# Transposes of the next tokens laid between value projections, and a first batch sorted in wider spaced pieces

## Chip, core and metric

The kernel runs on one core of a Trainium2 chip. The metric is the time of the device for one execution, in microseconds (us), as the median of several runs. PE is the matrix engine (PEld its loading of stationary operands), DVE the vector engine, ACT the scalar engine, POOL GpSimd and SP the engine whose queue issues most of the transfers (DMA). All arithmetic is in 32-bit floats.

## What is computed

Two images `x` of 256 channels and 56 x 56 pixels go through a non-local convolution block, and are then read as 2 batches of 3136 tokens of 256 values for a layer of causal attention and a layer of experts. The change lies in the second and third part.

```python
def reference(x, ...):
    x = conv_block(x, ...)                      # non-local block, ReLU, residual
    t = to_tokens(x)                            # (2, 3136, 256)
    # attention: 4 heads of 64, causal
    q, k, v = split(layernorm(t) @ W_attn)
    att = softmax(where(causal, q @ k.T / 8, min))
    t = t + (att @ v) @ W_proj
    # experts: each token goes to the best 2 of 8
    xf = layernorm(t)
    probs = softmax(xf @ gate_w + gate_b)       # (tokens, 8)
    cw = the two largest of probs, zero elsewhere
    t = t + sum_e cw[:, e] * (gelu(xf @ W1[e] + b1[e]) @ W2[e] + b2[e])
    return from_tokens(t)
```

## The kernel before

**One order for all engines.** In the attention stage the order of instructions is set by hand. Attention is cut into steps; there are 200 for each batch, one for each block of 448 queries, pair of heads and tile of 128 keys. Ahead of each step, `between` adds some other work: at every odd step two pieces from a queue (gate, output projection, sorting, scattering, loads), at every even one some pieces of the projections for the next queries. A piece is what a Python generator issues up to its next `yield`. `yield True` counts as a piece, `yield False` says that there is nothing to do now, and the next generator in the queue is asked.

```python
def pull(n=1):
    while n > 0:
        for g in list(queue):
            r = next(g, None)
            if r is None:
                queue.remove(g)
                break
            if r is not False:
                n -= 1
                break
        else:
            return

def between(i, left):            # left: steps to the end of this block of queries
    # ... loads of W2 at the very end
    tick[0] += 1
    if tick[0] % 2:
        pull(2)
        return
    nb, s = (b, i + 1) if i + 1 < NB else (b + 1, 0)
    if nb < B and s < NS and (nb == b or left < NCH - QB // P - 2):
        rest = max(0, PARTS * (s + 1) - at[nb] - 1)
        for _ in range(2 * -(-rest // max(2, left))):
            if at[nb] + 1 < PARTS * (s + 1):
                step(nb)
```

**The projections.** 512 tokens (4 tiles) at a time, as ten pieces: two of transposes (two tiles each), four of queries and keys, four of values. The rows are normalised on POOL one pair ahead, transposed on PE into a bank of PSUM, and copied by ACT to `px`, which has two halves. All results go through the same two banks (`tag="m"`, two buffers).

```python
pm = pool(whole, "m", bufs=2, space=PSUM)
bg = pool(whole, "bg", bufs=2)

def project_qkv(b, qT, kT, v, px):
    # todo: the pairs of tiles in order
    def normalise():
        # ...
        xn = bg.tile([P, 2, C], F32, tag="xn", ...)
        for a in range(m):
            nc.gpsimd.tensor_scalar(xn[:k, a], ts[b][:k, n + a, :C], mean, rstd, ALU.subtract, ALU.mult)
        ready[n] = xn

    normalise()
    for s in range(NS):
        # ...
        xT = px[:, s % 2]
        for n, m, k in pairs(first, end):                  # transposes
            xn = ready.pop(n)
            normalise()
            tp = bank(f"xp_{b}_{n}", (P, NH, 2 * P))
            # ... nc.tensor.transpose into tp
            nc.scalar.copy(xT[:, :, o : o + wp], tp[:, :, :wp])
            yield s
        for which in range(2):                             # queries, keys
            for hp in range(NH):
                ps = bank(f"qk_{b}_{s}_{which}_{hp}")
                # ... two matmuls with wat and xT
                nc.scalar.copy(to[:, s * QB : s * QB + w], ps[:, :w])
                yield s
        for n in range(first, end):                        # values
            ps = bank(f"v_{b}_{n}", (P, 512))
            # ... two matmuls with xT and wv, two copies by ACT
            yield s
```

The columns of `wv` beside the values hold the centred gate `gwc`, which two small matmuls (`gp`) and four DVE operations make before anything else of this layer. `wT`, which the gate needs once, takes a buffer of the tag `xn` too.

**The sorting** (`dispatch`) gives each token of a batch its place among the experts' blocks: some forty small DVE operations, a few at a time, with `small_piece` between them; then `hot` selects biases for `bp`, and each tile of rows is normalised by DVE (`xr`) and scattered to `x_slots` by two indirect transfers from POOL. The first batch is sorted during the attention of the second.

```python
def small_piece():
    yield True
    if b == 0:
        yield True
# ...
hot = g1.tile([E, w], F32, tag="hot", ...)
nc.vector.tensor_tensor(hot, eb[:E, :w], row.to_broadcast([E, w]), ALU.is_equal)
yield from small_piece()
if b:
    yield True
bp = bank(f"bp_{b}", (P, KH, w))
# ... matmuls of bp, a copy, small_piece
for n in range(NCH):
    # ... xr on DVE
    for k in range(2):
        nc.gpsimd.indirect_dma_start(out=xds[b], out_offset=idxs[b][:kk, k, n : n + 1], in_=xr[:kk], ...)
        yield True
        if b == 0:
            yield False
sent[b] = True
```

After its last scatter the first batch's queue loads `w1s`, in the place of that batch's rows, and the first rows for the experts (`xb_f_first`).

Of the kernel before, what the change touches and what calls it, by code (L numbers as in the profile page):

```python
# [13 lines left out]
ALU = mybir.AluOpType  # L14
# [13 lines left out]
def conv_attn_moe_kernel(  # L28
# [47 lines left out]
    nc = tc.nc  # L76
    P = 128
# [349 lines left out]
    def layer1(nm, general):  # L427

        with ExitStack() as whole:
# [7 lines left out]
            def bank(name, shape=(P, 512)):  # L437
                return pm.tile(list(shape), F32, tag="m", name=f"{name}_{nm}")


            gp = bank("gp")
            gpc = gp[:, :E]
            for c in range(NH):
                nc.tensor.matmul(gpc, ones, gw[:, c], start=(c == 0), stop=(c == NH - 1))
            for c in range(NH):
                nc.vector.scalar_tensor_tensor(gwc[:, c], gpc, -1.0 / C, gw[:, c], ALU.mult, ALU.add)
                nc.vector.tensor_copy(
                    wv[:, c, :, HS:], gwc[:, c].rearrange("p (h e) -> p h e", h=HEADS)
                )

            def project_gate():

# [20 lines left out]
            def project_qkv(b, qT, kT, v, px):  # L473

                todo = deque(p for s in range(NS) for p in pairs(s * QB // P, min(NCH, (s + 1) * QB // P)))
                ready = {}

                def normalise():
                    if not todo:
                        return  # L480
                    n, m, k = todo.popleft()
                    xn = bg.tile([P, 2, C], F32, tag="xn", name=f"xn_{nm}{b}_{n}")
                    for a in range(m):
                        nc.gpsimd.tensor_scalar(  # L484
                            xn[:k, a], ts[b][:k, n + a, :C],
                            ts[b][:k, n + a, MEAN : MEAN + 1], ts[b][:k, n + a, RSTD : RSTD + 1],
                            ALU.subtract, ALU.mult,
                        )
                    ready[n] = xn

                normalise()
                for s in range(NS):
                    w = min(QB, N - s * QB)
                    first, end = s * QB // P, -(-(s * QB + w) // P)
                    xT = px[:, s % 2]
                    for n, m, k in pairs(first, end):
                        xn = ready.pop(n)
                        normalise()
                        tp = bank(f"xp_{b}_{n}", (P, NH, 2 * P))
                        for a in range(m):  # L500
                            for c in range(NH):
                                nc.tensor.transpose(
                                    tp[:, c, a * P : a * P + k],
                                    xn[:k, a, c * P : (c + 1) * P],
                                    ident[:k, :k],
                                )
                        o, wp = n * P - s * QB, (m - 1) * P + k
                        nc.scalar.copy(xT[:, :, o : o + wp], tp[:, :, :wp])  # L508
                        yield s
                    for which in range(2):  # L510
                        for hp in range(NH):
                            ps = bank(f"qk_{b}_{s}_{which}_{hp}")
                            d0 = which * C + hp * P
                            for c in range(NH):
                                nc.tensor.matmul(  # L515
                                    ps[:, :w],
                                    wat[:, c, d0 : d0 + P],
                                    xT[:, c, :w],
                                    start=(c == 0),
                                    stop=(c == NH - 1),  # L520
                                )
                            to = kT[hp] if which else qT[:, hp]
                            nc.scalar.copy(to[:, s * QB : s * QB + w], ps[:, :w])
                            yield s
                    for n in range(first, end):
                        k = chunk(n)
                        ps = bank(f"v_{b}_{n}", (P, 512))
                        o = n * P - s * QB
                        for c in range(NH):
                            nc.tensor.matmul(  # L530
                                ps[:k, : C + E],
                                xT[:, c, o : o + k],
                                wv[:, c].rearrange("p h d -> p (h d)"),
                                start=(c == 0),
                                stop=(c == NH - 1),
                            )
                        half = (C + E) // NH
                        for hp in range(NH):
                            nc.scalar.copy(
                                v[hp][:k, n].rearrange("p a d -> p (a d)"),  # L540
                                ps[:k, hp * half : (hp + 1) * half],
                            )
                        yield s

                    full = [n for n in range(first, end) if chunk(n) == P]
                    for f, e, k in ((first, first + len(full), P), (first + len(full), end, chunk(end - 1))):
                        for hp in range(NH if f < e else 0):
                            c0 = C + 2 * hp * LH
                            nc.vector.tensor_tensor(
                                ts[b][:k, f:e, c0 : c0 + 2 * LH].rearrange("p n (a e) -> p n a e", a=2),  # L550
                                v[hp][:k, f:e, :, HS:],
                                ts[b][:k, f:e, SLOT : SLOT + 1].unsqueeze(3).to_broadcast(
                                    [k, e - f, 2, LH]
                                ),
                                ALU.mult,
                            )
                read[b] = True
# [349 lines left out]
            def dispatch(b):  # L907
# [5 lines left out]

                def small_piece():

                    yield True
                    if b == 0:
                        yield True

                def small(name, last=E, dt=F32):  # L920
# [172 lines left out]
                hot = g1.tile([E, w], F32, tag="hot", name=f"hot_{nm}{b}")  # L1093
                nc.vector.tensor_tensor(hot, eb[:E, :w], row.to_broadcast([E, w]), ALU.is_equal)
                yield from small_piece()
                if b:
                    yield True
                bp = bank(f"bp_{b}", (P, KH, w))
                for k in range(KH):
# [7 lines left out]
                for n in range(NCH):  # L1107
                    kk = chunk(n)
                    xr = (scatter_rows[0] if b else bg).tile(
                        [P, width], F32, tag="xr", name=f"xr_{nm}{b}_{n}"  # L1110
                    )
                    nc.vector.tensor_scalar(  # L1112
                        xr[:kk, :C], t[:kk, n, :C],
                        t[:kk, n, MEAN : MEAN + 1], t[:kk, n, RSTD : RSTD + 1],
                        ALU.subtract, ALU.mult,
                    )
                    if b:
                        nc.vector.tensor_copy(xr[:kk, C:], t[:kk, n, TOKEN : SLOT + 1])
                    for k in range(2):
                        s = nc.gpsimd.indirect_dma_start(  # L1120
                            out=xds[b],
                            out_offset=bass.IndirectOffsetOnAxis(ap=idxs[b][:kk, k, n : n + 1], axis=0),
                            in_=xr[:kk],
                            in_offset=None,
                            bounds_check=xds[b].shape[0] - 1,
                            oob_is_err=False,
                        )
                        group = f"x_slots_{nm}{b}"
                        tc.declare_no_dep(s.ins, group=group, reason="different rows")
                        tc.add_to_no_dep_group(group, s.ins)  # L1130
                        yield True
                        if b == 0:
                            yield False
                sent[b] = True

            def experts(w1s, w2s, b2s, ex, es, ps6, between, need, written):
# [343 lines left out]
            else:  # L1480
# [6 lines left out]
                finished = [[0] * NH for b in range(B)]  # L1487
                clock, later, tick = [0], [], [0]

                PARTS = QB // P // 2 + QB // P + 2 * NH  # L1490

                def step(b):
                    if next(pieces[b], None) is not None:
# [2 lines left out]
                    return False  # L1496

                def need(b, s):
                    while at[b] + 1 < PARTS * (s + 1) and step(b):
                        pass  # L1500

                att.enter_context(tc.manual_schedule(engines={PE, DVE, POOL, SP, ACT}))
                for b in range(B):
# [5 lines left out]
                    def between(i, left):  # L1509
# [10 lines left out]
                        nb, s = (b, i + 1) if i + 1 < NB else (b + 1, 0)  # L1520

                        if nb < B and s < NS and (nb == b or left < NCH - QB // P - 2):
                            rest = max(0, PARTS * (s + 1) - at[nb] - 1)
                            for _ in range(2 * -(-rest // max(2, left))):
                                if at[nb] + 1 < PARTS * (s + 1):
                                    step(nb)

                    due = attend(
# [128 lines left out]
```

## Time and profile before

| | |
|---|---|
| runs | 1390.78, 1390.88, 1399.16 us; median 1390.88 |
| span of the profiled execution | 1392.3 us, mean granted clock of PE 0.974 |
| convolution | up to about 93 us |
| attention with projections, both batches | 93 to 892 us |
| experts | 892 to 1350 us |
| the rest of the result | to 1392 us |

In the profile, L502 are the transposes (`xp_f`), L484 the normalisation on POOL (`xn_f`), L508 the copy to `px_f`, L515 the query and key projections (`qk_f`), L530 the value projections (`v_f`), L539 their copies; L621 the scores (`sc_f`), L629 the exponentials (`st_f`), L661 the weighted values (`yp_f`), L672 the last operation on a finished block (`qT_f`). L1100 is `bp`, L1120 the scatter, L1417 the load of `w1s`. A bracket behind an entry of the timeline is the idle time of the engine before it and what ended it; "granted clock" or PEclk is the share of PE's full clock. A wait is named as engine, what it was about to run, and what it waited for.

### The profile page before, as it was taken

How to read it: one execution, taken by the hardware profiler on the slowest of the kernel's cores; microseconds unless marked ns; L12 is line 12 of the kernel's file. 1: busy time of each engine (PE TensorE's matmuls, PEld its weight loads, DVE VectorE, ACT ScalarE, POOL GpSimd, SP SyncE). 2: the span in 40 equal slices, each digit the busy share in tenths (PEclk: the TensorE clock that was granted, in tenths of full speed). 3: DMA queues.
4: the chain of work that ended last, by engine and by line, in shares of the span. 5: the costliest groups of instructions: out<-in, count | busy, mean ns of one | idle time of the engine just before them, and what ended most of it. 6: DMA issues, size and time to landing. Idle time of an engine off the chain costs nothing. (4 is left out here: it accounts for less than half of the span.)

```text
span 1392.3 us, 27930 instructions
## 1 busy us (share of the span) xinstructions
PE 1306.3 (94%) x10642; PEld 824.4 (59%) x10642; DVE 789.5 (57%) x1634; ACT 613.3 (44%) x1247; POOL 314.4 (23%) x299
## 2 busy tenths in 40 slices
PE   8998999999999999999999999899888998999974
PEld 7874444444444444444444444489777998888872
DVE  1562555757777455677677878657333443444435
ACT  0244545545565554654445565543222332333322
POOL 1102101000000111110333440000563024655530
PEclk9999999999999999999999999999999999999995
DMA  9992001000000001000011134412333334344428
GB/s 309 381 318 76 23 19 26 23 16 16 16 9 23 8 2 37 17 8 16 30 42 46 52 92 158 132 53 61 123 126 103 106 99 139 122 131 145 124 74 260
DMA packets 110373, 123.94 MB, mean 89 GB/s; under 512 B 19423, under 2 KB 99948, under 8 KB 110232
## 3 DMA queue, kind: packets, MB, share of 16 engines
q1 hardware_dynamic: 92456, 89.67, 21.2%
q0 software_dynamic: 10416, 26.00, 5.5%
q10 hardware_dynamic: 7360, 6.39, 1.4%
q8 instruction: 88, 1.44, 0.4%
q14 instruction: 53, 0.43, 0.1%
HBM read 63.04 MB, written 60.81 MB: 89 GB/s over the span
## 5 line engine op out<-in xcount | busy, mean ns | idle before, releaser
L643 DVE TENSOR_TENSOR acc_f<-acc_f,st_f 128x896 f32<-128x896 f32 (+5 forms) x372 | 367.7, 988 | 166.4 <-ACT st_f L629 155.6
L629 ACT ACTIVATE st_f<-sc_f 128x896 f32<-128x896 f32 (+5 forms) x400 | 334.1, 838 | 286.2 <-PE sc_f L621 253.3
L661 PE MATMUL yp_f<-st_f,v_f 64*64 64x448 f32 (+6 forms) x3184 | 341.6, 505 | 7.1 <-DVE qT_f L672 5.7
L621 PE MATMUL sc_f<-qT_f,kT_f 64*64 64x448 f32 (+6 forms) x3184 | 342.0, 501 | 0.0
L1221 PE MATMUL ht_f<-xT_f,w_f 128*128 128x128 f32 x1680 | 215.4, 283 | 32.4 <-ACT xT_f L1202 24.7
L1230 ACT ACTIVATE g_f<-ht_f,b1b 128x128 f32<-128x128 f32 x420 | 120.1, 369 | 280.9 <-PE ht_f L1221 153.7
L1221 PEld LDWEIGHTS ht_f<-xT_f,w_f 128*128 128x128 f32 x1680 | 208.3, 197 | 46.0 <-ACT xT_f L1202 35.6
L621 PEld LDWEIGHTS sc_f<-qT_f,kT_f 64*64 64x64 f32 x3184 | 117.3, 133 | 151.9 <-issue 137.5
L661 PEld LDWEIGHTS yp_f<-st_f,v_f 64*64 64x64 f32 x3184 | 111.7, 133 | 157.5 <-issue 132.0
L484 POOL TENSOR_SCALAR xn_f<-t 128x256 f32<-128x256 f32 (+1 forms) x50 | 69.7, 1403 | 540.6 <-issue 325.2
L1120 POOL DMA_INDIRECT x_slots<-xr_f,idx x100 | 115.9, 1159 | 254.0 <-DVE xr_f L1112 144.0
L1209 DVE COPY w_f<-w1s_f 128x1024 f32 x105 | 73.5, 701 | 103.4 <-PE ht_f L1221 50.4
L1250 DVE TENSOR_TENSOR ys_f<-yp_f,kT_f 128x128 f32<-128x128 f32 x105 | 30.6, 291 | 122.1 <-PE yp_f L1240 102.9
L515 PE MATMUL qk_f<-px_f,wat 128*128 128x512 f32 (+1 forms) x224 | 95.1, 567 | 4.2 <-ACT px_f L508 4.2
L1257 POOL DMA_INDIRECT y_tokens<-ys_f,to_f x63 | 63.6, 1009 | 154.2 <-DVE ys_f L1250 143.9
L631 DVE TENSOR_TENSOR st_f<-st_f,keep 128x256 f32<-128x256 f32 (+1 forms) x112 | 43.5, 389 | 79.2 <-ACT st_f L629 64.7
L515 PEld LDWEIGHTS qk_f<-px_f,wat 128*128 128x128 f32 x224 | 39.2, 192 | 57.3 <-issue 45.0
L1240 PE MATMUL yp_f<-px_f,g_f 128*128 x210 | 64.6, 390 | 0.0
L1240 PE MATMUL yp_f<-kT_f,g_f 128*128 x210 | 64.0, 387 | 0.0
L1240 PE MATMUL yp_f<-v_f,g_f 128*128 x210 | 62.8, 381 | 0.0
L1240 PE MATMUL yp_f<-w2s_f,g_f 128*128 x210 | 62.5, 379 | 0.0
L1319 POOL DMA_INDIRECT y_f<-y_slots,idx x50 | 55.7, 1115 | 16.3 <-issue 14.9
(217 smaller groups left out, 1174.9 us busy)
## 6 DMA issues: line engine op xcount, KB each, us to landing
x_slots<-fill SPq DMA_DIRECT2D x1, 8127.0 KB
xb_f<-x_slots SPq DMA_DIRECT2D x21, 387.0 KB
x_slots<-fill SPq DMA_DIRECT2D x1, 7296.0 KB
y_slots<-ys_f SPq DMA_DIRECT2D x57, 128.0 KB
kept<-t SPq DMA_DIRECT2D x2, 3200.0 KB
x<-in_x_dram SPq DMA_DIRECT2D x14, 448.0 KB
xr<-in_x_rows_dram SPq DMA_DIRECT2D x12, 512.0 KB
y_f<-y_tokens SPq DMA_DIRECT2D x24, 256.0 KB
```

The costliest lines, as they stand in the source:

```text
L484: nc.gpsimd.tensor_scalar(xn[:k, a], ts[b][:k, n + a, :C], ts[b][:k, n + a, MEAN : MEAN + 1], ts[b][:k, n + a, RSTD : RSTD + 1], ALU.subtr ...
L515: nc.tensor.matmul(ps[:, :w], wat[:, c, d0 : d0 + P], xT[:, c, :w], start=(c == 0), stop=(c == NH - 1),)
L621: nc.tensor.matmul(ps[h : h + HS, a, c0:W], kT[hp][rows, j * P + h : j * P + h + HS], qT[rows, hp, q0 + c0 : q0 + W], start=True, stop=True,)
L629: nc.scalar.activation(st[:k, :, c0:], ps[:k, :, c0:W], AF.Exp, scale=SCALE)
L643: nc.vector.tensor_tensor(acc[:k, :, c0:], acc[:k, :, c0:], st[:k, :, c0:], ALU.add)
L661: nc.tensor.matmul(yp[a * HS : (a + 1) * HS, h // HS, c0:W], v[hp][h : h + HS, j, a, :HS], st[h : h + HS, a, c0:], start=first, stop=bool( ...
L1120: s = nc.gpsimd.indirect_dma_start(out=xds[b], out_offset=bass.IndirectOffsetOnAxis(ap=idxs[b][:kk, k, n : n + 1], axis=0), in_=xr[:kk], i ...
L1209: nc.vector.tensor_copy(w, w1s[:, :, bass.ds(e, 1), :].rearrange("p c e h -> p c (e h)"))
L1221: nc.tensor.matmul(ht[:, k, :], w[:, c, k * P : (k + 1) * P], xT[:, c, :], start=(c == 0), stop=(c == NH - 1),)
L1230: nc.scalar.activation(g[:, k, :], ht[:, k, :], AF.Gelu, bias=b1bs[b][:, k, i : i + 1])
L1240: nc.tensor.matmul(yp[:, :C], g[:, k, :], w2s[k][:, bass.ds(e, 1), :].rearrange("p e d -> p (e d)"), start=(k == 0), stop=(k == KH - 1),)
L1257: s = nc.gpsimd.indirect_dma_start(out=y_tokens, out_offset=bass.IndirectOffsetOnAxis(ap=to[:, n % GB : n % GB + 1], axis=0), in_=ys, in_o ...
```

## The change

It has three parts. The transposes of the next 512 tokens are taken out of the head of their own ten pieces and laid between the value projections of the present ones, one piece after the first value projection and one after the third; only the very first tokens are transposed ahead of everything. The aim is that normalised rows and copied transposes are there when they are read. With it the centring of the gate weights moves from the start of the layer to just ahead of the first value projections, and the count of pieces that must be done for a block (`upto`) follows the new order. Second, the sorting of the first batch gets three yields between its pieces in place of two, and three more between `hot` and `bp`, so that its DVE work is spread over more steps of attention. Third, the two scatters of one tile of rows are handed out in a row, with one turn for the rest of the queue after both and not after each.

```diff
-            gp = bank("gp")
-            # ... gwc and wv from gp
+            def centre_gate():
+                gp = bank("gp")
+                # ... the same
...
-                normalise()
-                for s in range(NS):
+                def transposes(s):
                     w = min(QB, N - s * QB)
-                    first, end = s * QB // P, -(-(s * QB + w) // P)
-                    xT = px[:, s % 2]
-                    for n, m, k in pairs(first, end):
+                    xT = xTs[s] = px[:, s % 2]
+                    for n, m, k in pairs(s * QB // P, -(-(s * QB + w) // P)):
                         xn = ready.pop(n)
                         normalise()
                         # ... transposes and copy
                         yield s
+
+                normalise()
+                xTs = {}
+                yield from transposes(0)
+                for s in range(NS):
+                    w = min(QB, N - s * QB)
+                    first, end = s * QB // P, -(-(s * QB + w) // P)
+                    xT = xTs.pop(s)
                     # ... queries and keys
+                    if b == 0 and s == 0:
+                        centre_gate()
+                    following = transposes(s + 1) if s + 1 < NS else iter(())
                     for n in range(first, end):
                         # ... values of tile n
                         yield s
+                        if (n - first) % 2 == 0 and next(following, None) is not None:
+                            yield s + 1
+                    for _ in following:
+                        yield s + 1
...
                 def small_piece():
-                    yield True
-                    if b == 0:
+                    for _ in range(1 if b else 3):
                         yield True
...
                 yield from small_piece()
-                if b:
+                for _ in range(1 if b else 3):
                     yield True
                 bp = bank(f"bp_{b}", (P, KH, w))
...
                         yield True
-                        if b == 0:
-                            yield False
+                    if b == 0:
+                        yield False
...
-                PARTS = QB // P // 2 + QB // P + 2 * NH
+                upto = list(range(NS))
+                for s in range(NS):
+                    tiles = min(NCH, (s + 1) * QB // P)
+                    ahead = min(NCH, (s + 2) * QB // P)
+                    upto[s] = len(list(pairs(0, ahead))) + 2 * NH * (s + 1) + tiles
+                upto[-1] += 1
...
-                            rest = max(0, PARTS * (s + 1) - at[nb] - 1)
+                            rest = max(0, upto[s] - at[nb] - 1)
                             for _ in range(2 * -(-rest // max(2, left))):
-                                if at[nb] + 1 < PARTS * (s + 1):
+                                if at[nb] + 1 < upto[s]:
                                     step(nb)
```

More of the change, by code (lines that the diff above doesn't have):

```diff
@@ L438, in bank @@
                 return pm.tile(list(shape), F32, tag="m", name=f"{name}_{nm}")
-            gp = bank("gp")
[L442 to L449, printed above, removed]
+            def centre_gate():
+                gp = bank("gp")
+                gpc = gp[:, :E]
+                for c in range(NH):
+                    nc.tensor.matmul(gpc, ones, gw[:, c], start=(c == 0), stop=(c == NH - 1))
+                for c in range(NH):
+                    nc.vector.scalar_tensor_tensor(gwc[:, c], gpc, -1.0 / C, gw[:, c], ALU.mult, ALU.add)
+                    nc.vector.tensor_copy(
+                        wv[:, c, :, HS:], gwc[:, c].rearrange("p (h e) -> p h e", h=HEADS)
+                    )
             def project_gate():
@@ L1498, in need @@
                 def need(b, s):
-                    while at[b] + 1 < PARTS * (s + 1) and step(b):
+                    while at[b] + 1 < upto[s] and step(b):
                         pass
```

## The prediction

> **What bounds the kernel now.** I read the page's busy times first, then busy time by stretch, then the waits of PE in the stretch that the change touches, then the timeline around the longest of them.
>
> ```profile
> PE 1306.3 (94%) x10642; PEld 824.4 (59%) x10642; DVE 789.5 (57%) x1634; ACT 613.3 (44%) x1247; POOL 314.4 (23%) x299
> ```
>
> PE is busy 94% of the span, so the kernel is as long as PE's work plus PE's idle time. A change that gives PE neither more nor less to do (this one) can only win idle time, or time lost at a lower clock. By stretch (columns: time, then PE, PEld, DVE, ACT, POOL, PEclk, DMA share, GB/s):
>
> ```profile
> 93.40:892.00 798.60, 779.64 (x7313) 349.86 (x7316) 524.86 (x856) 422.61 (x647) 127.98 (x96) 1.00 0.13 41
> 892.00:1350.00 458.00, 425.12 (x2830) 389.78 (x2822) 196.04 (x573) 162.97 (x547) 175.68 (x170) 0.97 0.36 110
> ```
>
> Attention with the projections of both batches is the first line: only 798.6 - 779.6 = 19 us of idle PE. The experts (second line) idle 33 us, but the change edits nothing there. So 19 us, and what the clock costs in that stretch, is the whole purse. Who ends PE's waits between 93 and 892 us (total, times, longest):
>
> ```profile
> PE yp_f L661 <- DVE qT_f L672: 5.7, 4, 1.7
> PE xp_f L502 <- POOL xn_f L484: 4.4, 4, 1.5
> PE qk_f L515 <- ACT px_f L508: 4.2, 5, 1.0
> PE bp_f L1100 <- DVE hot_f L1094: 1.7, 1, 1.7
> PE yp_f L661 <- DVE st_f L631: 0.9, 1, 0.9
> PE xp_f L502 <- ACT px_f L508: 0.8, 1, 0.8
> ```
>
> The transposes' own waits (xp_f for the normalised rows, qk_f for the copied transposes, xp_f for a bank) are 4.4 + 4.2 + 0.8 = 9.4 us. The sorting of the first batch owns bp_f's 1.7 and, by its place in the timeline, the 0.9. Part of the 5.7 belongs to it too: two of the four waits for qT_f, 3.2 us together, fall between 480 and 720 us. The timeline of PE at the start of attention:
>
> ```profile
> 108.72 0.66 PE L502 MATMUL xp_f<-ident,xn_f 128*128 128x128 f32 x4
> 110.85 0.44 PE L502 MATMUL xp_f<-ident,xn_f 128*128 128x128 f32 x2 [1.48 <-POOL xn_f L484]
> 112.55 0.44 PE L502 MATMUL xp_f<-ident,xn_f 128*128 128x128 f32 x2 [1.26 <-POOL xn_f L484]
> 113.66 5.40 PE L515 MATMUL qk_f<-px_f,wat 128*128 128x512 f32 x8 [0.67 <-ACT px_f L508]
> ```
>
> The reader should see two costs. The brackets are idle time: 1.48 + 1.26 + 0.67 = 3.4 us. And the eight matmul records of L515 take 5.40 us; the same eight take 3.70 elsewhere (at 503.07 and 609.98 in the same timeline). The window 113.7 to 119.1 shows a granted clock of 0.68. So the stall also cost 5.4 - 3.7 = 1.7 us of slow clock after it. The sorting shows the same pattern:
>
> ```profile
> 640.01 0.45 PE L661 MATMUL yp_f<-st_f,v_f 64*64 64x128 f32 x8 [0.88 <-DVE st_f L631]
> 640.28 0.93 PE L621 MATMUL sc_f<-qT_f,kT_f 64*64 64x448 f32 x8
> 642.95 1.32 PE L1100 MATMUL bp_f<-hot_f,b1s 8*128 8x42 f32 x8 [1.73 <-DVE hot_f L1094]
> 644.20 1.77 PE L661 MATMUL yp_f<-st_f,v_f 64*64 64x448 f32 x8
> ```
>
> 0.88 + 1.73 us idle within 3.6 us, and then L661 takes 1.77 us for what takes 0.93 to 0.98 elsewhere; the clock of 643.0 to 647.3 is 0.60.
>
> [...] Here all projections share two banks (tag m), and only 0.5 + 0.8 us of PE's waits look like a wait for such a bank. [...] at 671.14 POOL starts three normalisations directly behind a scatter, and PE waits 0.41 and 1.21 us for them.
>
> **The change, part by part.**
>
> 1. *Transposes ahead.* Nothing is added or removed: 100 transposes (14.8 us of PE), 26 ACT copies of about 0.58 us and 50 normalisations of 1.40 us on POOL stay. They move: tokens of piece s+1 are transposed after the first and third value projection of piece s. A value projection takes 2.05 us per two tiles, about 1 us each, so between two transpose pieces there are 2 us of PE work at least, and usually attention steps of 785 us / 400 = 1.96 us each (first score at 107.8, first expert transpose at 893.0, 400 steps). A pair's normalisation takes 2.4 to 3.2 us. It is emitted a whole piece ahead, so it is hidden. The query projections then find px written long before.
>    - Start of attention (107 to 119): the 3.4 us and the 1.7 us of clock go. What now waits? The four query/key projections follow the first scores at once; they share two banks, and ACT has the copy of wT, a table load (1.28 us) and an exponential (0.92) ahead of their copies. I put a new bank wait of 0.8 us there. Net 4.3.
>    - First piece: its own transposes still come first, with 0.81 and 0.68 us of wait; the bank that gp held is free, so I count 0.6 saved. The centring moves between the projections and the first values, and these read its result: gp is 0.61 us of PE as before, but then four DVE operations of 0.14 us with their hand-overs stand in the path, about 1.0 us. Net -0.4.
>    - The other three waits of qk_f for px_f (0.93 at 344, 0.98 at 503, 0.93 at 749): gone, 2.8; I count 2.5.
>    - The two waits at 673 and 675: 1.6.
>    - New: a transpose piece is 0.63 us, shorter than a value projection, so the value projection behind it may find its bank not yet copied out (0.44 us of copies plus some 0.3 us from PE's end to ACT's start). Some 0.1 us for each of 26: 2.5 us lost.
>    Sum: 4.3 - 0.4 + 2.5 + 1.6 - 2.5 = 5.5 us.
>
> 2. *Wider spacing of the sorting.* Counted through the code: before, 18 small pieces of two yields, and one, are 37 yields; two are drawn at every second attention step, so 37 steps from sort to scatter. After: 18 times three, one, and three more before bp: 58. The DVE chain (0.35 to 0.63 us an operation) is thinned by a third, and between hot and bp lie six steps, not two. bp's 1.73 us goes, the 0.88 mostly, and with them the clock's 1.7; of the 3.2 for qT_f I count 1.0. Sum 5.0 us.
>
> 3. *Scatter two at a time.* POOL already runs each row's two scatters back to back (0.3 us between), because only the first waits for DVE. So the cost doesn't move; the order of draws does. Before: one scatter for each draw, and the output projection of the second batch takes the other. After: two scatters and one projection in turn, so 25 tiles need 38 to 50 draws in place of 50. By my count the scatters run from step 82 to 162 of the second batch instead of 62 to 160: the later start is caught up. Value 0.
>
> Total 5.5 + 5.0 = 10.5 us: 1390.9 - 10.5 = 1380.4.
>
> **The rivals.** *The sort ends too late.* W1 takes the place of the first batch's rows, so it loads only after the last scatter:
>
> ```profile
> 831.49 1.18 POOL L1120 DMA_INDIRECT x_slots<-xr_f,idx  x1 [0.30 <-issue]
> 832.58 4.40 SPq L1417 DMA_DIRECT2D w1s_f<-in_w_dram  x8
> 837.34 1.41 SPq L1428 DMA_DIRECT2D xb_f_first<-x_slots  x2
> ```
>
> The experts start at 893, 55 us later. If the 21 steps of wider spacing were not caught up, W1 would be asked for some 41 us later (21 x 1.96), at 874, with 8 x 512 KB still to land; at the 153 GB/s that the window 800 to 850 shows, 27 us, so until 901: some 8 us lost, and the gain with them. My count gives two to four steps later (4 to 8 us), so I give it little weight. *A new wait takes the old one's place*: if PE waits for banks at every value projection (0.3 us each for 100), the gain of part 1 is gone: 1390. Against it: qk projections in a row use the same two banks today and hardly wait. *The two parts work, and the remaining qT_f waits fall too*: all 19 us less 5, and 3.4 of clock: 1373. *The experts shift phase*: the mean clock is 0.96, 0.92 and 0.98 in the hundreds from 900, 1000 and 1100 us, so there are dips among them; a different start may add or drop one, a few us either way.
>
> **Range and chances.** The purse of 19 + 3.4 us bounds the gain; 2% is 27.8 us, so more than 2% faster would need something outside attention. Slower by 2% needs W1 far later than I count. I take 1380.4 with about 9 us either way: 1371 to 1390. Faster 0.03, same 0.95, slower 0.02.
>
> **What would show it.** Right: no xp_f wait for xn_f and at most one qk_f wait for px_f; clock 1.00 from 105 to 892; no wait at bp_f; the window of attention with 8 to 11 us of idle PE and some 10 us shorter; W1 asked for 50 us ahead of the experts. Wrong: waits of v_f for its copies, or of the second scores' exponential, that sum to over 4 us; a wait for W1 at the experts' start; more clock dips among the experts.

## The result, and the profile after

| | before | after | ratio, 95% interval |
|---|---|---|---|
| first measurement | 1392.36 us (1390.78 to 1399.16) | 1379.42 us (1377.35 to 1381.16) | 0.9897, 0.986 to 0.9934 |
| again, beside the second group of experiments | 1353.51 us (1352.46 to 1355.71) | 1344.05 us (1341.66 to 1345.27) | 0.9919, 0.9905 to 0.9933 |

The change is about 1% faster: 12.9 us between the medians of the first measurement, 9.5 in the second, where the ratio stands for 11.0 us and the interval is narrower. (1392.36 is the median of four executions; the 1390.88 above was that of the first three.) The experiments ran in two groups, on two chips. On the second, which also measured the change again, the kernel before took 1353.51 us, on the first 1389.91. The kernel before was not profiled on the second, but the profiles of its variants show where such a difference lies: from the first expert transpose to the end they took 493 to 497 us on the first chip (transposes alone, sort alone and own wT, all described below), and 458 us on the second (the change and two of its variants). So ratios, not times, are to be compared across the groups.

The page of the changed kernel, and its busy time by stretch, with the limits laid at two events (end of the convolution, first transpose of the experts):

```profile
PE 1299.2 (94%) x10642; PEld 819.4 (60%) x10642; DVE 787.8 (57%) x1634; ACT 613.9 (45%) x1247; POOL 311.3 (23%) x299
...
94.10:884.00 789.90, 776.99 (x7317) 348.09 (x7317) 524.30 (x856) 422.94 (x648) 124.29 (x96) 1.00 0.14 42
884.00:1340.00 456.00, 420.90 (x2826) 386.45 (x2826) 196.84 (x576) 163.25 (x547) 177.13 (x171) 0.98 0.36 112
```

The same events lie at 93.4 and 893.0 us in the kernel before. So attention went from 799.5 us to 789.9. Of these 9.6 us, 6.3 were idle PE (19.2 us before, 12.9 after) and 3.4 were busy PE (780.4 and 777.0 us): the work is the same, so that part is matmuls that ran slower before. From the first expert transpose to the end of the span it was 1392.3 - 893.0 = 499.3 before and 1375.5 - 884.0 = 491.5 after, though the instructions there are the same. The last column but two is PE's clock: over 900 to 1300 us in hundreds it was 0.96, 0.92, 0.98 and 1.00 in the profile of before, and 0.98, 0.97, 0.97 and 1.00 after. (0.14 - 0.08) x 100 = 6 us of the 7.8 are thus clock. By the same sum the later profiles on the first chip, with the same experts, lose 8 or 9 us, not 14, so the profile of before was at the high end. I read only attention's share as the change's. Waits of PE in attention of the changed kernel (total, times, longest):

```profile
PE yp_f L677 <- DVE qT_f L688: 6.6, 5, 1.8
PE sp_f L704 <- ACT v_f L551: 2.5, 1, 2.5
PE qk_f L523 <- ACT px_f L508: 1.2, 1, 1.2
PE yp_f L677 <- DVE st_f L647: 0.6, 1, 0.6
PE v_f L542 <- DVE gwc L447: 0.6, 1, 0.6
```

The wait for normalised rows is gone, the wait for px_f is left once (the first tokens), bp has none. Two lines are new: v_f for the centred gate, 0.6 us, foreseen; and sp_f (the sums of a finished block) for a copy of v_f, 2.5 us, not foreseen at that place. The start of attention, timeline of PE:

```profile
109.74 0.60 PE L457 MATMUL wt_f<-ident,wpr 128*128 128x128 f32 x4
110.27 0.98 PE L637 MATMUL sc_f<-qT_f,kT_f 64*64 64x448 f32 x8
111.18 7.13 PE L523 MATMUL qk_f<-px_f,wat 128*128 128x512 f32 x16
118.25 0.77 PE L637 MATMUL sc_f<-qT_f,kT_f 64*64 64x320 f32 x8
```

No bracket stands here: the four projections (16 records) follow the first scores without a pause and take 7.13 us, at a granted clock of 1.00; before, eight records alone took 5.40, at 0.68. The first scatter came at 688.1 us (before: 651.5) and W1 was asked for at 827.7 us, 56 us ahead of the experts (before: 832.6, 60 ahead).

### The profile page after: what moved, and what is told of

Read it like the earlier page. It is cut to its first block, busy times and chain, and to the rows that moved or that the text cites. A ratio compares the mean times of both kernels' runs of the same rounds, so it can differ in the third digit from the quotient of the medians.

```text
span 1375.5 us, 27937 instructions
## 1 busy us (share of the span) xinstructions
PE 1299.2 (94%) x10642; PEld 819.4 (60%) x10642; DVE 787.8 (57%) x1634; ACT 613.9 (45%) x1247; POOL 311.3 (23%) x299
## 3 DMA queue, kind: packets, MB, share of 16 engines
q8 instruction: 88, 1.44, 0.4%
## 5 line engine op out<-in xcount | busy, mean ns | idle before, releaser
L1236 PE MATMUL ht_f<-xT_f,w_f 128*128 128x128 f32 x1680 | 213.0, 281 | 27.0 <-ACT xT_f L1217 17.4
```

Of the source, the lines that this page charges most:

```text
L1236: nc.tensor.matmul(ht[:, k, :], w[:, c, k * P : (k + 1) * P], xT[:, c, :], start=(c == 0), stop=(c == NH - 1),)
```

## The experiments

**Each part alone.** The first leaves the sorting and the scatter order as before; the second leaves the projections as before.

```diff
 # transposes ahead alone (against the changed kernel)
-                    for _ in range(1 if b else 3):
-                        yield True
+                    yield True
+                    if b == 0:
+                        yield True
 # ... and the gap ahead of bp and the scatter order likewise as before
```

> Part 1 alone: transposes ahead, centring moved, the sorting and the scatter order as before. Theory (sizes read from the two traces): PE's waits for normalised rows and transposes (9.4 us) shrink to 1.8, the clock dip at 114 us (1.7) goes, and one new wait of 2 us comes for a value copy held up behind the sort's exponential: attention 7.3 us shorter, about 1385 us. The waits at bp and the dip near 643 stay. Rival: most of the gain came from the sort's spacing, and this run wins 3 us or less (1389 or more).

```diff
 # sort and scatter alone (against the kernel before)
-                    yield True
-                    if b == 0:
+                    for _ in range(1 if b else 3):
                         yield True
 # ... and the gap ahead of bp and the scatter order as in the change
```

> Parts 2 and 3 alone: wider spacing and scatters two at a time, projections as before. Theory: bp's wait of 1.7 us and the dip of 1.7 go, 0.3 of st_f's wait, and 0.8 comes as a new wait for qT_f: attention 2.8 us shorter, about 1389.5 us; the waits at 109 to 114 us and the dip there stay; W1 is asked for within 10 us of the time before. Rival: the sort is what pays, 6 us or more (1386 or less).

Measured: transposes alone 1385.22 us against 1389.91, ratio 0.9967 (0.9949 to 0.9984); sort alone 1386.18, 0.9968 (0.9954 to 0.9981). By the medians the parts are worth 4.7 and 3.7 us. The intervals, 2.2 to 7.1 us and 2.6 to 6.4, do not quite shut out the rivals; the waits, which went as expected in both kernels, speak against them. The sum of the parts, 0.65%, counts 1.6 us (0.12%) twice, as shown below, and lies under the 0.81% of the whole; the intervals overlap. But transposes alone won only 3.8 us of attention in the profile (from the end of the convolution to the first expert transpose: 799.5 to 795.7), not 7.3. The timeline of that kernel shows why:

```profile
641.21 1.60 PE L1116 MATMUL bp_f<-hot_f,b1s 8*128 8x42 f32 x8 [1.73 <-DVE hot_f L1110]
642.74 1.77 PE L677 MATMUL yp_f<-st_f,v_f 64*64 64x448 f32 x8
644.29 1.72 PE L637 MATMUL sc_f<-qT_f,kT_f 64*64 64x448 f32 x8
```

bp's stall is the old one, but slow matmuls last longer behind it: the next scores take 1.72 and, at 646.84 us, 1.75 us, where 0.93 is usual; in the kernel before they took 1.58 and 0.98. Such a stretch of slow matmuls, with a low granted clock, is called a dip here. Another one follows the new wait of sp_f (granted clock 0.76 from 573 to 580 us). In the same way the stall at the start, left in place, cost the sort-alone kernel more than it cost before:

```profile
112.98 0.61 PE L502 MATMUL xp_f<-ident,xn_f 128*128 128x128 f32 x2 [1.26 <-POOL xn_f L484]
114.27 6.50 PE L515 MATMUL qk_f<-px_f,wat 128*128 128x512 f32 x8 [0.68 <-ACT px_f L508]
```

6.50 us for what took 5.40 before and takes 3.70 at a granted clock of 1.00 (at 503.07 and 609.98 us of the kernel before). The idle time of this stall is the same in both profiles within hundredths (1.48, 1.26 and 0.67 or 0.68 us); what the clock adds varies, here from 1.7 to 2.8 us.

The sort alone also lost the two waits for xn_f at 673 and 675 us: the scatters start at 693.1 us there, so that no normalisation stood behind one. Both parts remove these 1.6 us.

**Is the order of the scatters worth nothing?** The change, with the scatters handed out one at a time:

```diff
                         yield True
-                    if b == 0:
-                        yield False
+                        if b == 0:
+                            yield False
```

> The change with the scatters handed out one at a time as before. Theory: the wider spacing starts the scatters at step 82 and 50 draws put the last at step 182 of 200, so W1 (8 x 512 KB) is asked for at about 860 to 880 us and the first rows only at the end of attention; the experts start late by 5 to 10 us: 1385 to 1390, slower than the change. So the order of the scatters, worth nothing alone, pays for the spacing. Rival: transfers are quick enough to hide this too, and the time is that of the change, 1379.

Measured: 1402.75 us, 1.0088 (1.0063 to 1.0113) of the time before: 12.8 us slower than before, and more than expected. Attention was 795.6 us; from the first expert transpose to the end it took 514.1, 22.6 more than in the change. PE, then DVE, then the issuing queue of that kernel:

```profile
888.62 1.50 PE L586 MATMUL pp_f<-wpr,qT_f 128*128 128x264 f32 x6
907.46 1.25 PE L586 MATMUL pp_f<-wpr,qT_f 128*128 128x264 f32 x2 [17.34 <-DVE qT_f L736]
...
895.05 0.69 DVE L1224 COPY w_f<-w1s_f 128x1024 f32 x1 [8.28 <-DMA xb_f<-x_slots]
...
884.85 1.46 SPq L1432 DMA_DIRECT2D w1s_f<-in_w_dram  x3
```

W1's last issues come at 884.9, and the first copy of W1's weights starts at 895 after 8.3 us of waiting (the releaser named is a guess of the profile; the copy reads w1s). But a larger wait stands on PE: an output projection of the second batch, ahead of the first expert, waits 17.3 us for the scale of the last block of attention. While the first rows for the experts are not asked for, the kernel draws from the queue, and these draws brought projections forward whose scale was still on a round trip through memory: DVE waited 2.6 us for the transfer `sums<-sums` and 6.1 us for `rb_f<-inverses` ahead of making it.

**Which of the two costs?** The same kernel, with only the first batch's pieces drawn at that place:

```diff
                 while len(early_rows) < GB:
-                    pull()
+                    pull() if general else next(turns[0])   # turns[0]: the first batch's own pieces
```

> The kernel with wide spacing and single scatters that lost 22 us at the start of the experts, with one edit: while the first rows are not asked for, only the first batch's own pieces are drawn, and no output projections of the second batch. Theory: two costs came together. W1 landed about 8 us late (DVE's first copy of weights at 895), and the draws before the experts put an output projection ahead of the first expert, which then waited 17.3 us for the last block's scale, a round trip through memory. With the edit the second goes and the first stays: 10 to 13 us faster than that kernel, and 6 to 9 slower than the change. Rival: W1 alone was the cause and nothing is won.

Measured: 1354.39 us against 1353.51, 1.0005 (0.9997 to 1.0014). Against the change on the same chip that is 10.3 us slower, a little over the 6 to 9 expected; against the kernel without the edit, through the kernel before, some 11 to 12 us faster (1.0088 to 1.0005 of 1390 or 1354 us). The wait of 17.3 us is gone, and PE waits for the weights:

```profile
895.06 3.75 PE L1236 MATMUL ht_f<-xT_f,w_f 128*128 128x128 f32 x16 [6.74 <-DVE w_f L1224]
```

So both costs are real, and each about as large as the gain of the whole change. W1 late, with the slow matmuls behind it (3.75 us at 895.06 for what takes 2.05 at 905.57), sets the first experts back by 10.0 us against the change (21.7 us in place of 11.7 from the first transpose to the fourth group of ht_f), of which 7.6 are left at the end; the other 2.6 us of this kernel arise in attention (794.1 us against 791.5), where PE's waits are no longer than those of the change (11.7 us in all, against 11.9); slower matmuls are thus an estimate of their cause. Projections drawn too early cost 11 to 12.

**What made the transposes wait at the start?** In the kernel before, wT takes one of the two buffers of the normalised rows just then. One edit to the kernel before:

```diff
-                wT = bg.tile([P, NH, C], F32, tag="xn", name=f"wT_{nm}")
+                wT = gate_room[0].tile([P, NH, C], F32, tag="wT", name=f"wT_{nm}")   # a buffer of its own
```

> The kernel before, with one edit: wT gets a buffer of its own and no longer takes one of the two of xn. Theory: the stall at 109 to 114 us has two causes. The third pair of rows was normalised late since wT held its buffer: without that the two waits for xn_f (2.7 us) go. But the transposes still stand directly ahead of the projections, and ACT has a table load and an exponential ahead of their copies: the wait for px_f grows from 0.7 to about 2 us. Net 1.7 us, and 1.7 more if the clock dip goes: 1389 to 1391. Rival 1: the order alone is the cause, no gain. Rival 2: the shared buffer is all of it, and the full 5.1 us come (1387).

Measured: 1389.07 us, 0.999 (0.9973 to 1.0006), not told apart from the kernel before by time; attention in the profile 797.9 us, 1.6 shorter. The timeline shows the two causes apart:

```profile
108.43 1.09 PE L504 MATMUL xp_f<-ident,xn_f 128*128 128x128 f32 x8
111.46 3.70 PE L517 MATMUL qk_f<-px_f,wat 128*128 128x512 f32 x8 [1.93 <-ACT px_f L510]
```

Both pairs are transposed in one go, so the late rows came from the shared buffer; yet the projections then wait 1.93 us, for copies behind a table load and an exponential on ACT (1.28 and 0.92 us in the profile of before). In these runs that second wait is gone only with the new order. No dip followed here (3.70 us, at a granted clock of 1.00 from 112 to 119 us). Yet attention kept only the shorter waits, 3.41 - 1.93 = 1.5 us: by these numbers the 1.7 us of the old dip were lost again elsewhere in attention, an estimate, and where was not shown. By the timeline both rivals fail: the waits for rows are gone, and not all of the stall is.

**The new wait.** In the changed kernel ACT's timeline around 572 us reads:

```profile
571.30 0.37 ACT L951 ACTIVATE lg_f<-lg_f 128x200 f32<-128x200 f32 x1 [3.14 <-DVE lg_f L950]
571.58 0.90 ACT L645 ACTIVATE st_f<-sc_f 128x896 f32<-128x896 f32 x1
572.38 0.43 ACT L551 COPY v_f<-v_f 128x132 f32<-128x132 f32 x2
572.69 0.61 ACT L508 COPY px_f<-xp_f 128x512 f32<-128x512 f32 x1
```

The sort's exponential (L951) stands 3.14 us at the head of ACT's queue until DVE has its input, and the copies that free PE's banks stand behind it. The edit to the changed kernel puts a piece between:

```diff
                 nc.vector.tensor_tensor(pr, pr, wide(red), ALU.subtract)
+                yield from small_piece()
                 nc.scalar.activation(pr, pr, AF.Exp)
```

> The change with one more small piece between the sort's first DVE operations and its exponential on ACT. Theory: the one new wait of the change, 2.5 us of sp_f for the copy of v_f at 573 us, came since ACT, in order, stood 3.1 us before that exponential, which waited for DVE, with v_f's and px_f's copies behind it. Given three more yields the exponential finds its input there and the wait goes: 2 us shorter than the change. Scatters and W1 come 2 to 3 steps later, some 5 us, with 50 to spare. Rival: the wait comes from the transposes' bank, and stays.

Measured: 1341.21 us (1339.65 to 1342.28), 0.9905 (0.9891 to 0.9918) of the time before, against 1344.05 for the change on the same chip: 2.8 us by the medians. The wait of sp_f is gone (2.5 us), and so is the dip behind it (some 1.7): behind sp_f the weighted values take 0.98 and 0.93 us, where they took 1.44 and 1.70 in the change; st_f's waits grew from 0.6 to 1.7. Attention took 788.1 us against 791.5. The exponential runs without a wait:

```profile
572.23 0.36 ACT L952 ACTIVATE lg_f<-lg_f 128x200 f32<-128x200 f32 x1
```

This version has the lowest time of the study, though its interval and that of the change overlap by a little.

**Spacing or gap?** The change with two yields between the small pieces, as before, but with the three ahead of bp:

```diff
-                    for _ in range(1 if b else 3):
-                        yield True
+                    yield True
+                    if b == 0:
+                        yield True
```

> The change with the old spacing of the small pieces (two yields), but the three yields ahead of bp kept. Theory: bp's wait (1.7 us) and the clock dip it caused (1.7) are all that the sort's part is worth, and the gap alone removes them: the time of the change within 1 us, with W1 asked for some 30 us earlier. Rival: the wider spacing itself pays, by fewer waits of yp_f for qT_f and st_f: 2 to 3 us slower than the change.

Measured: 1344.46 us, 0.9926 (0.9912 to 0.9939), within 0.4 us of the change; W1 is asked for from 803.0 us on, in place of 827.1, though the last of its eight loads at 825.8 us, in place of 830.8. So the wider spacing shows no gain that can be told from noise, and the gap between hot and bp, with the order of the scatters, brings most of what the sort's part is worth. The intervals leave room for some 2 us: in its one profile this kernel's attention takes 793.6 us, 2.1 more than the change, of which a dip at 594 us makes 1.6 (1.77 and 1.72 us for two groups that take 0.93 each).

**The change again,** beside these kernels:

> The change itself, measured again beside the kernels of this call. Theory: the two parts alone gave 0.9967 and 0.9968 of the time before; together 0.9935, some 9 us; the 13 us of the first measurement held some luck among the experts (their clock dips cost 13.7 us in the profile of before and 8.5 in most others). Rival: the parts help each other, and it is 0.990 again.

Measured: 0.9919 (0.9905 to 0.9933), or 11.0 us, with medians 9.5 us apart. That lies between the theory's 0.9935 and the rival's 0.990, and the interval ends just short of both, so it decides for neither. Attention took 791.5 us from the end of the convolution to the first expert transpose, where the first profile of the change had 789.9.

## Why the prediction was right

It gave 1380.4 us and a gain of 10.5; measured were 1379.42, and gains of 12.9 and 9.5. The bound was read rightly: all that the change could win lay in the idle PE of attention and two clock dips. Of the 10.5, 3.4 were the two dips and 7.1 idle PE; the first profile shows 6.3 and 3.4, 9.6 in all, and the second, where one new dip stands, 8.0. That the first time fell within 1 us of the forecast is in part luck: its 12.9 us hold some from the experts, and in the sum two errors nearly cancel: by the terms below the transposes are worth 6.8 us and not 5.5, the sort 2.8 and not 5.0, as long as no new dip comes.

*Transposes ahead, 5.5 us predicted.* Measured alone, 4.7, with the new dip in its profile. The terms: 4.3 at the start of attention was 5.1, since the bank wait of 0.8 that the prediction put there didn't come: all four projections run without a pause. The first piece, -0.4: from the end of the convolution to the first values 10.2 us became 10.4, so -0.2; the wait for the gate is 0.55 us, not 1.0, and px_f's is 1.20. The three other waits for px_f went (2.8). The two at 673 and 675 went, but the sort's part alone removes them too. The new bank waits, -2.5, have the right size for the wrong reason, which is luck: no value projection waits for its bank behind a transpose. The 2.5 us are one wait, behind the sort's exponential on ACT; the experiment that moved the exponential shows it.

*Sort, 5.0 us predicted.* Measured alone, 3.7, with the 1.6 above in it. bp's 1.73 and the dip behind it went as said. The wait for st_f at 640 us went, but one of 0.62 us came at 600.7. The 1.0 us for qT_f failed: the total rose from 5.7 to 6.6. The prediction took two of its waits, 3.2 us, for the sort's by their place in time; but the same 1.49 us stands at 134.7 us, where nothing is sorted, and both are still there after the change (1.49 us at 517.1, 1.76 at 590.9). The rise is a fifth wait, just behind the old place of bp:

```profile
642.03 1.73 PE L677 MATMUL yp_f<-st_f,v_f 64*64 64x448 f32 x16 [0.80 <-DVE qT_f L688]
```

In the kernel before, bp's stall and the slow matmuls behind it held PE up until this operation's input was there (DVE starts to make it at 646.60 us, and PE comes to it at 648.58). The wait stands in all seven profiles without the stall (0.42 to 1.06 us), with wide and with old spacing, and in none of the three with it. So of bp's 1.73 us some 0.8 came back here.

*Scatter order, value 0.* Alone it was not tried. In the change it is worth far more, since it is what catches the later start up: without it the kernel is slower than before. The rival "the sort ends too late" was sized at 8 us and the gain with it; late W1 costs 8 to 10, and the projections drawn ahead of the experts, which the prediction hadn't seen, 11 to 12 more. The count of steps held: the scatters began 37 us later (41 was the estimate), ended at 830.7 us, and W1 was issued 56 us ahead of the experts, as without the change to within 4 us.

*Clock.* The mean of the whole stretch is no test, since it is 1.00 before too; windows of 3.5 us tell more. In them the two old dips (0.51 from 114.6 to 118.1 us and 0.59 from 643.0 to 646.5) are gone, and the first profile of the change has none (1.00 in every such window of attention), as predicted. But the second has one just behind the 2.5 us wait of sp_f. The same window in the first and in the second, with the clock third from the end:

```profile
573.00:580.00 7.00, 7.00 (x76) 3.58 (x75) 4.34 (x8) 3.41 (x9) 0.00 (x0) 1.00 0.01 1
573.00:580.00 7.00, 7.00 (x48) 3.32 (x51) 3.92 (x8) 2.81 (x7) 0.00 (x0) 0.76 0.01 1
```

The four variants that kept that wait have the dip as well (0.76 to 0.83). Of the later profiles, the one with the exponential moved has none there (0.98 and 0.93 us for the weighted values, as above). So in five of the six profiles with the new wait a dip came behind it; what sets one off was not shown. The dip adds to the cost of the wait, and the step that failed here is the one that took the new waits for many small ones.

## What to carry to other kernels

Work of other stages that is laid between the pieces of the bounding engine should be handed out so that an instruction's input is ready when its engine comes to it (ACT stood 3.14 us before one exponential here, with the copies for PE behind it): the piece that computes an input and the piece that uses it belong apart. That gap paid here, while a wide spacing of everything showed no gain of its own. A stall that goes can lay bare a smaller one behind it (0.8 us behind bp's 1.73). Before spreading work out, count where its last transfer will fall and what is loaded behind it: room that seems ample can be lost by a single change in the order of draws. Judge stalls of PE by idle time and by the slow matmuls behind them together (3.4 us idle and 1.7 to 2.8 us of slow matmuls at the start of attention), and a difference in an unchanged stage by several profiles.

## What was not expected of the hardware

Matmuls behind a stall ran slow in some executions and not in others, with the same idle time to within hundredths: behind sp_f's wait of 2.52 us the clock was 1.00 in one profile of the change and 0.76 in the other, and behind the stall at the start of attention the same eight records took 5.40 us in one kernel and 6.50 in another. And the two chips differ by 2.6% on the kernel before (1389.91 and 1353.51 us). Busy time by stretch of the change on the faster one:

```profile
93.60:885.10 791.50, 778.67 (x7317) 348.89 (x7316) 524.51 (x856) 423.02 (x648) 125.45 (x96) 1.00 0.14 42
885.10:1310.00 424.90, 409.52 (x2830) 381.23 (x2830) 200.20 (x582) 163.44 (x548) 182.23 (x171) 0.99 0.40 123
```

Attention is 1.6 us longer than in the first profile of the change, about what its dip costs. From the experts to the end it takes 458.4 us in place of 491.5; PE's wait for xT_f falls from 17.4 to 5.9 us and the clock between 985 and 1285 us is 1.00. Whether it is the chip that makes the experts stall more in the other profiles was not settled.
